# Beta as a row of the matmuls that fill the last stage's accumulators, in place of thirteen additions among the experts

## The chip, the cores and the metric

The kernel runs on one core of a Trainium2 chip. The metric is the device time of one execution in microseconds. It was timed in three runs before the change.

Five engines work beside each other, each through its own queue of instructions in order: TensorE (PE, matrix products into the accumulators of PSUM), VectorE (DVE), ScalarE (ACT), GpSimd (POOL) and SyncE (SP), which in this kernel issues most of the transfers. GpSimd issues the indirect ones (gathers and scattered writes).

## The reference

One layer of a graph network with a mixture of experts, a batch norm, a residual and a layer norm. There are 6250 nodes with 256 features, 200,000 edges and 64 experts.

```
h    = x * rsqrt(deg_out);  m = segment_sum(h[src], dst) * rsqrt(deg_in)
x1   = m @ W_gc + b_gc + (x @ W_res + b_res)
core = top-2 mixture of 64 experts of x1 (gelu between two layers, gates by softmax)
y    = x1 + core
mean, var = of y over the nodes
bn   = (y - mean) * rsqrt(var + 1e-5) * gamma + beta
out  = layernorm(x + bn)          # over the 256 features
```

`beta` has 256 values, one for each feature, and is added to every node's row.

## The kernel before, in words

The nodes stand in NT = 50 tiles of TP = 125 rows. Three parts follow one another: the sum over the edges (about 0 to 930 us of the profiled execution), the experts (about 990 to 1441 us, with the gating ahead of them), and the final stage (to 1544 us).

**The experts' stage.** `slotted()` has one loop over the 64 experts, e = -1 to 63. Iteration e does the first layer of expert e+1, the transposes for e+2 and the second layer of e:

- TensorE makes `ph` from `xgT` and `w1s` (L1647), and ScalarE takes it through gelu into `hT` (L1649).
- Rows of nodes are gathered four experts ahead, into `xg` (GpSimd, L1605). TensorE transposes them into `pte` (L1627), VectorE copies this into `xgT` (L1630), and picks the gates with small instructions `two` (L1636).
- VectorE subtracts `c` from one tile of x1 (`room`, L1758; both inputs lie in SBUF) and adds the tile to `x_sum` (L1759).
- The second layer gives `py` (L1663); VectorE adds the bias (`yb`, L1673). Some experts go by columns: `ph` (L1685), `yT` on VectorE (L1686), `py` (L1692).
- ScalarE scales by the gate (`ys`, L1701, six buffers), VectorE adds to `y_sum` (L1702), and GpSimd writes the rows to `y_dram` at scattered places. The page gives all indirect transfers of this stage one line, L1605; they are told apart by their tiles.
- `ahead(e)` lets SP issue the loads: the next experts' weights (`w1s` L1242, `w2s` L1252, `b2s`; VectorE copies the biases, `bc`, L1244), tiles of x1, and, at e % 4 == 2, four tiles of the kernel's input into `fb` (`node_in`, L212). `fb` holds the residual x for the final stage: 128 partitions by 50 tiles by 256.

At e == 3 SP also brings `beta`, repeated on 125 partitions, into the tile `bet`. From e = 5 on, at e % 4 == 1, GpSimd adds `bet` to the four tiles of `fb` that a load has brought before (L1774), 13 times in all.

The order on TensorE, ScalarE, VectorE and SP is the order in which this stage's code is written. GpSimd's is not: the scheduler puts its instructions in a row, except that all gathers, and each expert's first write, keep the program's order among themselves.

**The final stage.** After the experts, `y_dram` comes back in `yr`, is added to x1 (VectorE), and the sums over nodes give `mean`, `scale` and `less` = mean * scale. `shifted(t, whole)` (L1987) then brings tiles of `fb` into accumulators `pf` by a matmul with the stationary matrix `unit`: the identity in its first 125 rows, and -1 in the rows from 125 on. For the tiles from 12 on, a DMA has put `less`, repeated, into partition 125 of `fb` (L2041), and the matmul reads 126 rows: so pf = fb + beta - less, beta being in `fb` already. For the first 12 tiles the matmul runs ahead of `less`, with 125 rows, and `less` is subtracted by a second one. VectorE adds `pf` to the scaled tiles, and the layer norm follows.

`unit` is made by GpSimd ahead of the experts (L1480 and L1481).

Of the kernel before, what the change touches and what calls it, by code (L numbers as in the profile page):

```python
# [9 lines left out]
F32 = mybir.dt.float32  # L10
# [6 lines left out]
ALU = mybir.AluOpType  # L17
# [9 lines left out]
TP = 125  # L27
NT = N // TP
# [3 lines left out]
D = 256  # L32
# [140 lines left out]
def gnn_moe_kernel(ctx, tc, x_in, x_cols, src, dst, bases, nexts, firsts, parts, lasts, W_gc, b_gc, W_res, b_res, Wg, bg, w1, b1, w2, b2,  # L173
                   gamma, beta, out):
    nc = tc.nc
    V, S, G, T = nc.vector, nc.scalar, nc.gpsimd, nc.tensor
# [6 lines left out]
    def node_rows(ap, t0, n):  # L183
        return ap[t0 * TP:(t0 + n) * TP, :].rearrange("(t p) d -> p t d", p=TP)
# [13 lines left out]
    def node_dma(eng, to_sbuf, tile_ap, rows):  # L198

        for a, b in ((0, 112), (112, TP)):  # L200
            if to_sbuf:
                loads.append(eng.dma_start(out=tile_ap[a:b], in_=rows[a:b]))
            else:
                eng.dma_start(out=rows[a:b], in_=tile_ap[a:b])

    def node_in(tile_ap, ap, t0, n, end=NT):

        if t0 + n in (end, NT):
            node_dma(nc.sync, True, tile_ap[:TP, n - 1:n], node_rows(ap, t0 + n - 1, 1))
            n -= 1  # L210
        if n:
            loads.append(nc.sync.dma_start(out=tile_ap[:, :n], in_=bass.AP(  # L212
                tensor=ap.tensor, offset=ap.offset + t0 * TP * ap.ap[0][0],
                ap=[[ap.ap[0][0], 128], [TP * ap.ap[0][0], n], [1, ap.shape[1]]])))

    def bcast_rows(ap, n):
        return ap.rearrange("(o d) -> o d", o=1).to_broadcast([n, ap.shape[0]])
# [21 lines left out]
    ident = const.tile([128, 128], F32, name="ident")  # L239
# [8 lines left out]
    pidx = const.tile([128, 1], F32, name="pidx")  # L248
# [100 lines left out]
    with tc.tile_pool(name="edges", bufs=1) as ep, ExitStack() as later:  # L349
        iota_h = ep.tile([128, NS * WMAX, 2], FP16, name="iota_h")  # L350
        for a in range(0, NS * WMAX, 128):
            b = min(a + 128, NS * WMAX)
            V.tensor_scalar(iota_h[:, a:b, :], iota_f[:, :b - a, None].to_broadcast([128, b - a, 2]), float(a), None,
                            op0=ALU.add)
# [64 lines left out]
        with tc.tile_pool(name="late", bufs=1) as lp, tc.tile_pool(name="both", bufs=2) as bp, \  # L419
# [33 lines left out]
            for k, w in enumerate((W_gc, W_res)):  # L453
                nc.sync.dma_start(out=wcat[:, :, k * D:(k + 1) * D],
                                  in_=w.rearrange("(k p) d -> p k d", p=128))
# [200 lines left out]
            for i in range(NGR // CG):  # L656
# [55 lines left out]
                if i % 6 == 0 and 6 <= i <= 42:  # L712
                    r = i // 6 * 7
                    nc.sync.dma_start(out=z_dram[0:6272, :].rearrange("(p r) d -> p r d", p=128)[:, r - 7:r, :],
                                        in_=zeros[:, None, :].to_broadcast([128, 7, D + 2]))
# [30 lines left out]
        with tc.tile_pool(name="xs", bufs=1) as xs, tc.tile_pool(name="hotg", bufs=2) as hg, \  # L746
# [417 lines left out]
            now, n = 0.0, 0  # L1164
# [47 lines left out]
    unit = rpool.tile([128, TP], F32, name="unit")  # L1212
    below = rpool.tile([128, 1], F32, name="below")
# [67 lines left out]
    with tc.tile_pool(name="ps_r", bufs=1, space=PSUM) as ps_r, tc.manual_schedule():  # L1281
# [7 lines left out]
        for t0 in range(ta, tb, 4):  # L1289
            n = min(4, tb - t0)  # L1290
# [5 lines left out]
        for t0 in range(0, NL, 4):  # L1296
            n = min(4, NL - t0)
# [135 lines left out]
        for t0 in range(tb, NT, 10):  # L1433
            n = min(10, NT - t0)
# [23 lines left out]
        for k, h in enumerate(HAVE):  # L1458
# [6 lines left out]
                               op1=ALU.mult, accum_out=slots_of)  # L1465
# [11 lines left out]
        G.tensor_copy(dump8, dump[:, :FULL])  # L1477
        G.memset(y_sum, 0.0)
        G.memset(x_sum, 0.0)
        G.tensor_scalar(below, pidx, float(TP), -1.0, op0=ALU.is_ge, op1=ALU.mult)  # L1480
        G.tensor_scalar(unit, ident[:, :TP], below, None, op0=ALU.add)  # L1481
        G.memset(minus, -1.0)

        by_place(1, 0, E)
# [92 lines left out]
    fpool = ctx.enter_context(tc.tile_pool(name="fpool", bufs=1))  # L1577
    fb = fpool.tile([128, NT, D], F32, name="fb")
    gam = fpool.tile([TP, D], F32, name="gam")
    bet = fpool.tile([TP, D], F32, name="bet")  # L1580
    with tc.tile_pool(name="ex", bufs=2) as xp, \
            tc.tile_pool(name="ps_t", bufs=1, space=PSUM) as ps_t, \
            tc.tile_pool(name="ps_h", bufs=4, space=PSUM) as ps_h, \
# [4 lines left out]
        def settled():  # L1588
            while late:
                late.pop(0)()  # L1590
# [19 lines left out]
        def rows_in(idc, m, static=True):  # L1610

            xgs = []
            for k, at in enumerate(idc):
                n = min(128, m - k * 128)
                xg = gx.tile([128, D + 2], F32, name="xg")
                kept(static)(out=xg[:n], out_offset=None, in_=x_dram[:, :],
                             in_offset=bass.IndirectOffsetOnAxis(ap=at[:n], axis=0))
                xgs.append(xg)
            return xgs
# [100 lines left out]
        def columns(tab, e):  # L1720
            c, n, m = _place(turns[e])
            return [tab[:, c + k:c + k + 1] for k in range(n)]

        def turned(e, xgs):
            c, n, m = _place(turns[e])
            return turned_in(xgs, slots_of_turn[e], [mine_of[:, c + k, :] for k in range(n)], columns(gate_of, e),
                             () if e else owners)
# [3 lines left out]
        def slotted():  # L1731

            rows = [rows_in(columns(ids, e), slots_of_turn[e]) for e in range(EARLY)]
            xgTs = [turned(0, rows[0])]
            hTs = []
            for e in range(-1, E):
                if e >= 0:
                    ahead(e)
                if 0 <= e < E - EARLY:
                    rows.append(rows_in(columns(ids, e + EARLY), slots_of_turn[e + EARLY]))  # L1740
                first, second, sides = [], [], []
                if e + 1 < E:
                    hT, first = first_layer(*firsts_of[e + 1], xgTs[e + 1], slots_of_turn[e + 1])
                    hTs.append(hT)
                if e >= 0 and turns[e] in by_columns:
                    sides, second = second_layer_columns(seconds_of[e][0], firsts_of[e][1], hTs[e], columns(dest, e),
                                                         columns(gate_of, e), slots_of_turn[e])
                elif e >= 0:
                    second = second_layer(*seconds_of[e], hTs[e], columns(dest, e), columns(gate_of, e), slots_of_turn[e],
                                          True, e == E - 1)  # L1750
                for run in first[:2]:
                    run()
                    settled()
                if e + 2 < E:
                    xgTs.append(turned(e + 2, rows[e + 2]))
                if 0 <= e < NT:
                    xe = x(tb + e if e < NT - tb else ta + e - NT + tb if e < NT - ta else e - NT + ta)
                    V.tensor_tensor(xe, xe, c0, ALU.subtract)  # L1758
                    V.tensor_tensor(x_sum, x_sum, xe, ALU.add)  # L1759
                if sides:  # L1760
                    n = 1 if len(second) > 2 else 2
                    for run in sides + first[2:2 + n] + second[:2] + first[2 + n:] + second[2:]:
                        run()
                    first, second = [], []
                for k in range(4):
                    for run in second[k:k + 1]:
                        run()
                    for run in first[2 + k:3 + k]:
                        run()
                        settled()  # L1770
                if e % 4 == 1 and e > 4 and e // 4 * 4 - 4 < NT:
                    t0 = e // 4 * 4 - 4
                    n = min(4, NT - t0)
                    G.tensor_tensor(fb[:TP, t0:t0 + n, :], fb[:TP, t0:t0 + n, :],  # L1774
                                    bet[:, None, :].to_broadcast([TP, n, D]), ALU.add)

        def ahead(e):
            if e % 3 == 1 and e // 3 * 3 < ta:
                t0 = e // 3 * 3
                n = min(3, ta - t0)  # L1780
                node_in(x_all(t0, n), x_rows, t0, n, ta)
            if e == 3:
                nc.sync.dma_start(out=bet, in_=bcast_rows(beta, TP))
                nc.sync.dma_start(out=gam, in_=bcast_rows(gamma, TP))
            if e % 4 == 2:
                t0 = e // 4 * 4
                n = min(4, NT - t0)
                if n > 0:
                    node_in(fb[:, t0:t0 + n, :], x_in, t0, n)
            if 2 < e + 2 < E:  # L1790
                r = turns[e + 2]
                seconds_of.append(second_weights(order[0:1, r:r + 1], r not in by_columns))
            if e + 3 < E:
                firsts_of.append(first_weights(order[0:1, turns[e + 3]:turns[e + 3] + 1]))
# [9 lines left out]
    with tc.For_i(0, n_again, 1), tc.tile_pool(name="all", bufs=1) as ap, \  # L1804
# [7 lines left out]
        whole = 2 * N // 128  # L1812
        for r in range(0, whole, 8):
            n = min(8, whole - r)
            nc.sync.dma_start(out=y_dram[0:128 * whole, :].rearrange("(p r) d -> p r d", p=128)[:, r:r + n, :],
                              in_=zeros[:, None, :].to_broadcast([128, n, D]))
# [3 lines left out]
        with tc.For_i(0, n_groups, 1) as gi:  # L1820
# [6 lines left out]
                            op1=ALU.mult)  # L1827
# [3 lines left out]
                                   op0=ALU.mult, op1=ALU.add)  # L1831
# [22 lines left out]
            with tc.For_i(0, n_win, 1):  # L1854
# [17 lines left out]
                                     in_=res, in_offset=None, compute_op=ALU.add)  # L1872
# [100 lines left out]
    with tc.tile_pool(name="fin", bufs=1) as fp, tc.tile_pool(name="gat", bufs=4) as gp, \  # L1973
# [9 lines left out]
        def shifted(t, whole):  # L1983

            pf[t] = ps_f.tile([TP, 2, D], F32, name="pf")
            n = TP + 1 if whole else TP
            T.matmul(pf[t], unit[:n, :], fb[:n, t:t + 2, :], start=True, stop=whole)  # L1987

        pm = ps_m.tile([TP, D], F32, name="pm")
# [3 lines left out]
        for t in range(0, 6, 2):  # L1993
            shifted(t, False)
# [25 lines left out]
        t0 = 0  # L2020
# [16 lines left out]
        less = fp.tile([TP, D], F32, name="less")  # L2037
        V.tensor_mul(less, mean, scale)


        nc.sync.dma_start(out=fb[TP:TP + 1, 12:, :], in_=less[0:1, None, :].to_broadcast([1, NT - 12, D]))  # L2041
        for t in range(0, 12, 2):
            T.matmul(pf[t], minus, less[0:1, None, :].to_broadcast([1, 2, D]), start=False, stop=True)  # L2043

# [1 line left out]
        groups, t0 = [], 0  # L2046
# [113 lines left out]
```

## Time and profile before

| | |
|---|---|
| median of 3 runs | 1558.65 us (1556.74 to 1560.66) |
| profiled execution | 1545.78 us |
| its span | 1544.1 us |
| mean granted clock of TensorE | 0.957 |
| TensorE, VectorE, ScalarE, GpSimd busy | 1374.5, 1094.7, 802.1, 790.0 us |
| TensorE's idle time, 990 to 1441 us | 31.6 us (the sum over its lines) |
| additions of `bet` to `fb` (L1774) | 13, 29.5 us of GpSimd, from 1009.8 to 1357.9 us |

The durations in the text come from the profiled execution; the result will stand against the median of the runs, 12.9 us (0.8%) above it. Rows of the timeline give start and duration, then the engine, line, operation and tiles; the bracket at their end is the engine's idle time before the row and what ended it. Rows of the groups give total, mean duration and the idle time before. Rows of the waits give total, count and longest.

### The profile page before, as it was taken

The page shows a single profiled execution, that of the slowest core. Times are in us where ns is not written, and L with a number is a line of the kernel's source. Part 1 is how long each engine was busy: PE and PEld are TensorE (multiplying, and loading weights), DVE is VectorE, ACT ScalarE, POOL GpSimd, SP SyncE. Part 2 cuts the span into 40 slices and gives each one's busy share as a digit, 9 for nine tenths or more (in the row PEclk, how much of TensorE's full clock was granted, in tenths as well). Part 3 has the DMA queues.
Part 4 walks back from the last instruction along what each step waited for, and adds up shares of the span by engine and source line. Part 5 has one row for each costly group of instructions (what it writes and reads, how often), then busy time and mean ns, then how long its engine had stood idle before and what let it go on. Part 6 is the DMA issues. An engine that isn't in the chain of part 4 may idle for free. (4 is left out here: it accounts for less than half of the span.)

```text
span 1544.1 us, 32496 instructions
## 1 busy us (share of the span) xinstructions
PE 1374.5 (89%) x9814; PEld 1143.0 (74%) x9814; DVE 1094.7 (71%) x3328; ACT 802.1 (52%) x2127; POOL 790.0 (51%) x900
## 2 busy tenths in 40 slices
PE   8998577899999999999999987799999988998783
PEld 4555466777888989899999985688778877787541
DVE  9999976888888877777767579455544455433587
ACT  7887634567766666565555534333333333333258
POOL 4000256776676667666676632366556666554100
PEclk9999688999999999999999999999999999999897
DMA  6765856666677777777777747688797866576645
GB/s 199 210 210 158 315 167 187 195 193 194 182 205 217 197 218 204 202 216 212 224 201 200 199 133 197 157 252 264 231 279 236 252 212 212 187 222 209 220 161 156
DMA packets 197857, 319.84 MB, mean 207 GB/s; under 512 B 27245, under 2 KB 129442, under 8 KB 197673
## 3 DMA queue, kind: packets, MB, share of 16 engines
q1 hardware_dynamic: 143308, 170.57, 35.2%
q0 software_dynamic: 47888, 146.88, 33.2%
q10 hardware_dynamic: 6477, 0.24, 0.6%
q8 instruction: 79, 1.29, 0.3%
q14 instruction: 105, 0.86, 0.2%
HBM read 250.79 MB, written 60.35 MB: 202 GB/s over the span
## 5 line engine op out<-in xcount | busy, mean ns | idle before, releaser
L766 POOL DMA_INDIRECT r<-h_dram,srcg x445 | 481.2, 1081 | 259.6 <-PE pc L857 90.2
L912 PE MATMUL sm<-hrow,room 128*128 128x258 f32 x1470 | 492.3, 349 | 8.9 <-DVE room L900 7.3
L877 ACT CAST room<-pc 128x196 f32 (+7 forms) x879 | 356.6, 406 | 221.1 <-PE pc L857 117.6
L913 PE MATMUL sm<-hrow,room 128*128 128x256 f32 x1470 | 397.1, 283 | 0.0
L857 PE MATMUL pc<-hotk,lo 128*128 128x245 bf16 (+7 forms) x1118 | 308.3, 308 | 42.3 <-issue 16.4
L835 DVE TENSOR_TENSOR hotk<-key,iota_h 128x784 bf16<-128x784 f16 (+4 forms) x488 | 248.0, 508 | 136.0 <-PE pc L857 90.0
L912 PEld LDWEIGHTS sm<-hrow,room 128*128 128x128 f32 x1470 | 289.5, 197 | 27.4 <-issue 18.7
L913 PEld LDWEIGHTS sm<-hrow,room 128*128 128x128 f32 x1470 | 282.2, 192 | 1.3
L1649 ACT ACTIVATE hT<-ph,bc 128x112 f32<-128x112 f32 (+16 forms) x256 | 106.0, 425 | 286.6 <-PE ph L1647 143.2
L1647 PE MATMUL ph<-xgT,w1s 128*128 128x112 f32 (+17 forms) x1024 | 208.0, 348 | 9.6 <-ACT hT L1649 4.7
L900 DVE TENSOR_TENSOR room<-pc,room 128x49 f32 x908 | 197.0, 239 | 18.5 <-issue 6.2
L1647 PEld LDWEIGHTS ph<-xgT,w1s 128*128 128x128 f32 x1024 | 171.2, 198 | 31.8 <-issue 10.0
L1605 POOL DMA_INDIRECT y_dram<-ys,dest x124 | 120.0, 968 | 145.5 <-ACT ys L1701 101.5
L1605 POOL DMA_INDIRECT xg<-x_dram,ids x124 | 118.5, 956 | 83.6 <-issue 66.8
L771 PE MATMUL pg<-r,hot 128*128 128x258 f32 x445 | 146.9, 330 | 11.5 <-ACT resg L1154 5.0
L857 PEld LDWEIGHTS <-lo 128*128 128x128 bf16 x1118 | 100.7, 102 | 72.2 <-issue 16.5
L1630 DVE TENSOR_SCALAR xgT<-pte,bsum 128x112 f32<-128x112 f32 (+14 forms) x128 | 48.7, 421 | 111.7 <-PE pte L1627 40.1
L772 PE MATMUL pg<-r,hot 128*128 128x256 f32 x445 | 126.6, 285 | 0.0
L1663 PE MATMUL py<-w2s,hT 128*128 128x256 f32 (+3 forms) x424 | 107.0, 396 | 7.0 <-DVE y_sum L1702 4.1
L771 PEld LDWEIGHTS pg<-r,hot 128*128 128x128 f32 x445 | 86.9, 195 | 23.4 <-issue 11.4
L1685 PE MATMUL ph<-hT,w2s 128*128 128x208 f32 (+9 forms) x480 | 98.9, 358 | 2.2 <-issue 1.7
L384 DVE TENSOR_TENSOR lo<-lo_b,iota 128x1024 bf16<-128x1024 bf16 x140 | 96.0, 686 | 5.1 <-PE pc L857 4.4
(373 smaller groups left out, 2006.2 us busy)
## 6 DMA issues: line engine op xcount, KB each, us to landing
w1s<-in_L_gnn_w_dram SPq DMA_DIRECT2D x64, 512.0 KB
w2s<-in_L_gnn_w_dram SPq DMA_DIRECT2D x64, 512.0 KB
yr<-y_dram SPq DMA_DIRECT2D x10, 1024.0 KB
h_dram<-hrow SPq DMA_DIRECT2D x5, 1536.0 KB
r<-h_dram,srcg POOLq DMA_INDIRECT x445
f<-in_x_cols_dram SPq DMA_DIRECT2D x25, 256.0 KB
z_dram<-zeros SPq DMA_DIRECT2D x7, 903.0 KB
r_dram<-hx SPq DMA_DIRECT2D x24, 256.0 KB
```

The source lines that it names most:

```text
L766: G.indirect_dma_start(out=f32(r[:, :2 * D]), out_offset=None, in_=h_dram[:, :], in_offset=bass.IndirectOffsetOnAxis(ap=idx, axis=0))
L771: T.matmul(pg, hot, r[:, D:], start=first, stop=False)
L772: T.matmul(pg[:, :D], hot, r[:, :D], start=False, stop=last)
L835: V.tensor_tensor(hot, pairs(key, e, n, m), iota_h[:, None, :m, :].to_broadcast([128, n // 2, m, 2]), ALU.is_equal)
L857: T.matmul(pc, los[g // PAIRS][:, r // 2, :, r % 2], hots.pop(g), start=(i == 0), stop=(i == k - 1))
L877: put = S.copy(counts[c % 2][:, :, 1:][:, :, ds(at, w - 1)], pc[:, :, 1:])
L900: add = V.tensor_tensor(to, more, f32(had), ALU.add).ins
L912: T.matmul(sm, by, hrow[:, t, D:], start=(t == 0), stop=False)
L913: T.matmul(sm[:, :D], by, hrow[:, t, :D], start=False, stop=(t == NS - 1))
L1605: w = G.indirect_dma_start(**kw)
L1647: T.matmul(ph[:, :m], w1s[:, kk, c * 128:(c + 1) * 128], xgT[:, kk, :m], start=(kk == 0), stop=(kk == 1))
L1663: T.matmul(py[:n], hT[:, c, k * 128:k * 128 + n], w2s[:, c, :], start=(c == 0), stop=(c == 3))
```

## The change

`beta` becomes a row of `fb`, beside the shift's row. `unit` gets a row of +1 at 125 and -1 from 126 on, beside the identity; since `ident` has no entry in its 125 columns there, it is now made of a comparison and an addition. At e == 53, after the last load of `fb`, SP copies `beta` fifty times into partition 125. The shift's row `less` goes to partition 126. The matmuls read 126 rows for the first 12 tiles and 127 for the others. The tile `bet`, its load and the 13 additions go.

```diff
-        G.tensor_scalar(below, pidx, float(TP), -1.0, op0=ALU.is_ge, op1=ALU.mult)
-        G.tensor_scalar(unit, ident[:, :TP], below, None, op0=ALU.add)
+        G.tensor_scalar(below, pidx, float(TP + 1), -2.0, op0=ALU.is_ge, op1=ALU.mult)
+        G.tensor_scalar(unit, pidx.to_broadcast([128, TP]), float(TP), below, op0=ALU.is_ge, op1=ALU.add)
+        G.tensor_tensor(unit, unit, ident[:, :TP], ALU.add)
...
-    bet = fpool.tile([TP, D], F32, name="bet")
...
-                if e % 4 == 1 and e > 4 and e // 4 * 4 - 4 < NT:
-                    t0 = e // 4 * 4 - 4
-                    n = min(4, NT - t0)
-                    G.tensor_tensor(fb[:TP, t0:t0 + n, :], fb[:TP, t0:t0 + n, :],
-                                    bet[:, None, :].to_broadcast([TP, n, D]), ALU.add)
...
             if e == 3:
-                nc.sync.dma_start(out=bet, in_=bcast_rows(beta, TP))
                 nc.sync.dma_start(out=gam, in_=bcast_rows(gamma, TP))
...
+            if e == NT + 3:
+                nc.sync.dma_start(out=fb[TP:TP + 1], in_=beta[None, None, :].to_broadcast([1, NT, D]))
...
-            n = TP + 1 if whole else TP
+            n = TP + 2 if whole else TP + 1
...
-        nc.sync.dma_start(out=fb[TP:TP + 1, 12:, :], in_=less[0:1, None, :].to_broadcast([1, NT - 12, D]))
+        nc.sync.dma_start(out=fb[TP + 1:TP + 2, 12:, :], in_=less[0:1, None, :].to_broadcast([1, NT - 12, D]))
```

The order of the instructions on TensorE, VectorE and ScalarE stays as it was. GpSimd's changes in the experts' stage. Before, around the second addition:

```order
L1605 DMA xg<-x_dram,ids 128x258 x2
L1605 DMA xg<-x_dram,ids 96x258
L1605 DMA xg<-x_dram,ids 128x258
L1605 DMA xg<-x_dram,ids 112x258
L1605 DMA y_dram<-ys,dest 28372x256
L1774 TENSOR_TENSOR fb<-fb,bet 125x1024
L1605 DMA y_dram<-ys,dest 28372x256 x2
```

Now, at the same place (`xg` rows are gathers, `y_dram` rows the experts' scattered writes):

```order
L1605 DMA xg<-x_dram,ids 128x258 x2
L1605 DMA xg<-x_dram,ids 96x258
L1605 DMA y_dram<-ys,dest 28372x256
L1605 DMA xg<-x_dram,ids 128x258
L1605 DMA xg<-x_dram,ids 112x258
L1605 DMA y_dram<-ys,dest 28372x256 x2
```

The addition is gone, and one write that stood behind two gathers now stands ahead of them. Over the stage 12 gathers have one or two more writes ahead of them than before, and some 55 have fewer. A later place on the same engine, as a difference:

```order
 L1605 DMA xg<-x_dram,ids 112x258
+L1605 DMA y_dram<-ys,dest 28372x256 x2
 L1605 DMA xg<-x_dram,ids 128x258
 L1605 DMA xg<-x_dram,ids 48x258
-L1774 TENSOR_TENSOR fb<-fb,bet 125x1024
-L1605 DMA y_dram<-ys,dest 28372x256 x6
+L1605 DMA y_dram<-ys,dest 28372x256 x4
```

Two of six writes that came in a row behind the addition have moved ahead of two gathers.

SP's queue has one entry less at e == 3 and one more at e == 53, `fb<-beta`, between two weight loads:

```order
L1242 DMA w1s<-in_L_gnn_w_dram 128x2x512
L1785 DMA fb<-in_L_gnn_beta_dram 1x50x256
L1249 TENSOR_LOAD order
L1252 ISA
L1252 DMA w2s<-in_L_gnn_w_dram 128x4x256
```

The copy stands directly ahead of the next expert's load of `w2s`.

## The prediction

> **What bounds the kernel now.** I read the page's head first, then the stretches of the program, then the groups of the lines that the change touches, and last the rows around each addition.
>
> ```profile
> span 1544.1 us, 32496 instructions
> PE 1374.5 (89%) x9814; PEld 1143.0 (74%) x9814; DVE 1094.7 (71%) x3328; ACT 802.1 (52%) x2127; POOL 790.0 (51%) x900
> core 0: us, PE busy (x) PEld busy (x) DVE busy (x) ACT busy (x) POOL busy (x), PEclk, DMA share, GB/s
> 1050.00:1110.00 60.00, 59.84 (x289) 47.35 (x288) 30.87 (x99) 21.37 (x49) 36.23 (x35) 1.00 0.76 242
> 1290.00:1350.00 60.00, 52.99 (x290) 42.95 (x289) 30.01 (x101) 19.31 (x48) 32.83 (x33) 0.97 0.60 191
> ```
>
> TensorE is busy in 89% of the span. The two lower rows (windows of the span; after the length, busy time by engine) lie in the experts' stage, where all the additions are: in the first stretch TensorE hardly pauses, in the second it loses 7 of 60 us, VectorE and GpSimd work about half the time, and the transfers take 60 to 76%. So an instruction taken off GpSimd helps only if TensorE waited for it, directly or through another engine.
>
> ```profile
> L1774 POOL TENSOR_TENSOR fb<-fb,bet 125x1024 f32<-125x1024 f32 (+1 forms) x13 | 29.5, 2271 | 9.1 <-DMA fb<-in_x_dram 7.7 <-issue 1.2
> POOL y_dram L1605 <- ACT ys L1701: 101.5, 40, 7.0
> 1440.62 3.08 DMA y_dram<-ys,dest
> ```
>
> The 13 additions hold GpSimd for 29.5 us. But in the same stage GpSimd waits 101.5 us, in 40 places, for ScalarE's `ys`: its queue is in step with the results, not behind. The chain that ended last runs, from the experts on, through the last write of `y_dram`, which GpSimd can't issue before the last expert's `ys` exists. Taken by themselves the additions are hidden by these 101.5 us.
>
> **What the additions do to VectorE.** The stretch behind the second addition:
>
> ```profile
> 1034.15 0.15 DVE L1636 SCALAR_TENSOR_TENSOR two<-xg,mine_of 128x2 f32<-128x2 f32 x1
> 1034.22 3.31 DVE L1758 TENSOR_TENSOR room<-room,c 125x256 f32<-125x256 f32 x1
> 1034.87 2.37 POOL L1774 TENSOR_TENSOR fb<-fb,bet 125x1024 f32<-125x1024 f32 x1
> 1037.91 0.42 DVE L1673 TENSOR_TENSOR yb<-py,b2s 128x256 f32<-128x256 f32 x1
> 1038.38 1.63 PE L1663 MATMUL py<-w2s,hT 128*128 128x256 f32 x3 [1.11 <-DVE yb L1673]
> ```
>
> The subtraction of `c`, whose two inputs both lie in SBUF, takes 3.31 us and ends 0.3 us after the addition; undisturbed it takes 0.42 (1265.91 below). VectorE stood still for 2.9 us, `yb` came late, and TensorE waited 1.11 us for it. The tenth addition:
>
> ```profile
> 1263.60 2.36 POOL L1774 TENSOR_TENSOR fb<-fb,bet 125x1024 f32<-125x1024 f32 x1
> 1264.19 1.79 DVE L1636 SCALAR_TENSOR_TENSOR two<-xg,mine_of 112x2 f32<-112x2 f32 x1
> 1265.91 0.42 DVE L1758 TENSOR_TENSOR room<-room,c 125x256 f32<-125x256 f32 x1
> 1266.71 0.73 DVE L1686 TENSOR_SCALAR yT<-ph,bc 128x192 f32<-128x192 f32 x2
> 1267.17 1.23 PE L1692 MATMUL py<-ident,yT 128*128 128x128 f32 x4 [3.48 <-DVE yT L1686]
> ```
>
> Here a `two` takes 1.79 us instead of 0.15, so 1.64 of TensorE's wait of 3.48 is the standstill's; the other 1.84 has another cause. Other standstills reach nobody:
>
> ```profile
> 1009.70 2.52 DVE L1636 SCALAR_TENSOR_TENSOR two<-xg,mine_of 128x2 f32<-128x2 f32 x1
> 1010.77 1.03 PE L1647 MATMUL ph<-xgT,w1s 128*128 128x256 f32 x4
> 1289.89 2.77 DVE L1244 COPY bc<-bT 128x6 f32 x1
> 1292.97 0.47 DVE L1702 SCALAR_TENSOR_TENSOR y_sum<-py,gate_of,y_sum 32x256 f32<-32x256 f32 x1 [0.32 <-ACT ys L1701]
> ```
>
> During the first, TensorE runs on without a wait (no bracket at 1010.77); after the second, VectorE itself waits for ScalarE soon, so it had caught up.
>
> **What else stands beside the additions.** Not every gap there is theirs:
>
> ```profile
> 1116.37 0.46 SPq L212 DMA_DIRECT2D fb<-in_x_dram  x1
> 1121.04 0.45 ACT L1649 ACTIVATE hT<-ph,bc 128x224 f32<-128x224 f32 x1 [1.53 <-PE pte L1627]
> 1125.14 2.35 POOL L1774 TENSOR_TENSOR fb<-fb,bet 125x1024 f32<-125x1024 f32 x1
> 1127.31 2.95 PE L1647 MATMUL ph<-xgT,w1s 128*128 128x224 f32 x7 [2.37 <-ACT hT L1649]
> 1208.58 2.00 PE L1663 MATMUL py<-w2s,hT 128*112 128x256 f32 x5 [2.02 <-DVE y_sum L1702]
> ...
> 1100.00:1110.00 10.00, 10.00 (x57) 8.91 (x56) 5.40 (x16) 3.99 (x10) 6.11 (x7) 1.00 0.48 166
> 1117.00:1127.00 10.00, 7.95 (x49) 7.02 (x47) 1.86 (x6) 2.03 (x6) 8.15 (x8) 1.00 0.98 318
> ```
>
> Each addition works on four tiles of `fb` that one load has brought shortly before; here SP issued it 8.8 us ahead of the addition. After the load the DMA engines are full (0.98 against 0.48), VectorE and ScalarE fall to 2 us of work in ten, and `hT` is already late at 1121.04, four microseconds before the addition. That load stays, so I count the 2.37 at 1127.31 and, by the same picture, the 2.02 at 1208.58 to the transfers. The clock is the last piece (columns: the window, its length, PE busy, granted clock, share of the DMA engines, GB/s):
>
> ```profile
> 1038.40:1041.80 3.40, 3.40 (x8) 0.51 0.81 259
> 1127.20:1130.60 3.40, 3.29 (x10) 0.50 1.03 333
> 1209.10:1212.50 3.40, 3.40 (x10) 0.50 0.53 195
> 1267.10:1270.50 3.40, 3.33 (x17) 0.50 0.83 305
> 1304.70:1308.10 3.40, 3.36 (x14) 0.50 0.74 235
> 1359.30:1366.10 6.80, 6.28 (x23) 0.50 0.53 185
> ```
>
> These six windows at half the granted clock each follow a wait of TensorE; 1304.7 has no addition near it. TensorE is busy all through them, so a window of 3.40 us costs 1.7.
>
> **The change, part by part.**
> - The additions go: 29.5 us of GpSimd, nothing on the path but the standstills. Term: −1.1 (1034) and −1.64 (1263), together −2.7. The rest I take at nothing, for the two reasons shown (TensorE has queued work, or VectorE has slack).
> - The half-clock windows: behind the gap of 1.11 at 1038.38, which goes whole, the window should go: −1.7. At 1267.17 a wait of 1.84 remains, longer than the 1.11 that sufficed at 1038, so I leave that window in place. Bounds 0 and −3.4. The Trainium skill ("TensorE: Matmul & The Clock Gate", "HAM oscillation — how this bites in real kernels") asks only that TensorE have no idle gap above some 3.4 us; by that a gap of 1.11 couldn't halve the clock, and this term would be nothing, with a sum of about −2.7. The trace differs: the half clock begins at 1038.40, right behind the 1.11, and I follow the trace.
> - The load of `bet` (125 rows of 1 KB) goes; the row of `beta` (50 pieces of 1 KB) comes in at iteration 53. Both lie among transfers that leave the DMA engines room (0.60 to 0.76 above), and the row is needed only a stage later, where its semaphore has long been counted up. Taken as nothing. For the bounds I let the load's issue (0.39, below) and the shift's (0.73, the nearest row to a copy into one partition) stand on SP's path: −0.4 to +0.7.
> - `unit` takes one GpSimd instruction more, at most as long as the one before (0.64, below), in the preparation ahead of the experts. GpSimd's next task there is descriptors for the first gathers; cover is TensorE's remaining work of that stage. Nothing; upper bound +0.6.
> - The matmuls read one more row each:
>
> ```profile
> L1987 PE MATMUL pf<-fb,unit x50: 592/592/1217, 1447.6 to 1525.0; 126*125 126x512 f32 x38, 125*125 125x512 f32 x12
> L1783 SPq DMA_DIRECT2D bet<-in_L_gnn_beta_dram x1: 393/393/393, 999.7 to 999.7; - x1
> L2041 SPq DMA_DIRECT2D fb<-less x1: 727/727/727, 1492.3 to 1492.3; - x1
> L1481 POOL TENSOR_SCALAR unit<-ident,below x1: 636/636/636, 934.5 to 934.5; 128x125 f32<-128x125 f32 x1
> ```
>
>   125 and 126 rows together have a lowest and a middle duration of 592 ns, so the row is free: 0. The shift's row moves from partition 125 to 126 with the same 38 pieces: 0.
> - GpSimd's queue is put in another order: without the additions its writes of `y_dram` and gathers of `xg` stand differently to each other. Twelve gathers have one or two more writes ahead of them, some fifty fewer. Behind such a write, which waits for ScalarE, the gather waits too, and behind the gather TensorE's transposes (`pte`). Taken as nothing on this row:
>
> ```profile
> PE pte L1627 <- DMA xg<-x_dram,ids: 0.2, 1, 0.2
> ```
>
>   TensorE waited for a gather once, 0.2 us, in the whole stage; they are issued four experts ahead. The other end is the rival below.
>
> Sum: −2.7 − 1.7 = −4.4. The profiled execution took 1545.78 us with the 1.7 around its span, and would come to 1541.4. It lies 12.9 us under the median of the runs, 1558.65, which is what the result will be held against; the stage's gain is the same there, so 1558.65 − 4.4 = 1554.3.
>
> **The rivals.**
> - *More than the two standstills* (larger gain). All the gaps at the additions are theirs, since VectorE's backlog lasts longer than the trace tells: 1.11 + 3.48 + 2.37 + 2.02 = 9.0 from the rows above, and five of the windows (all but 1304.7), 4 × 1.7 + 3.4 = 10.2: up to −19, about 1539.5; with half of it −9.6, 1549. For it: five windows lie right behind additions. Against: `hT` was late before the addition came, and at 1127 no VectorE instruction ran beyond its length.
> - *Nothing.* The stage is paced by the transfers, and what TensorE no longer waits for VectorE, it waits for weights or `hT` some matmuls later: 1558.65, within 2. For it: the 1.84 left at 1267, and the DMA share of 0.98 behind the load at 1116. Against: in the stretch 1050 to 1110 the transfers leave a quarter free and TensorE doesn't wait.
> - *Slower, through GpSimd's new order.* A write that stands ahead of a gather waits 101.5/40 = 2.5 us in the mean, 7.0 at most. If the twelve gathers were late by it and a third came through to `pte`, that is 4 × 2.5 = 10 us, less the −4.4 of the standstills: +5.6, 1564; with none of the gain, +10, 1568.7. It decides from the point where a gather lands after its transposes could start, of which the 0.2 us is so far the only sign.
>
> **How the numbers follow.** Chances: the forecast (−1 to −7: from the 1.1 alone to 2.7 + 3.4 + 0.4) 0.50, more 0.20, nothing 0.15, slower 0.12, something not thought of 0.03. The likeliest case's own range is 1551.7 to 1557.7. For 8 in 10 I leave out the far half of the larger gain (below 1542) and most of the slower case (above 1563): 1542 to 1563. What a measurement can tell from no change is 0.3%, 4.7 us. The forecast's centre lies just inside; some 0.4 of its chance is beyond it: 0.20 for faster, with 0.20 from the larger gain: 0.40. Within: 0.30 + 0.15 + 0.02 = 0.47. Slower: 0.12 and 0.01.
>
> **What would show it.** Right: no `room`, `two` or `bc` on VectorE above 1 us in the stage; no wait for `yb` near 1038, no half clock there; the waits behind the loads of `fb` (near 1127, 1208) still there; PE's wait for `xg` still under 1 us. Wrong: these waits gone too (then they were the additions'), waits of `pte` for `xg` of several microseconds (GpSimd's order), or a new gap elsewhere that takes back the 4.4.

## The result, and the profile after

The changed kernel took 1551.61 us in the median of 12 runs (1541.18 to 1557.15), the kernel before 1558.39 in 12 runs on the same chip. The ratio is 0.9941, with a 95% interval of 0.9924 to 0.9958: 9.2 us faster, between 6.5 and 11.8 (the two medians alone differ by 6.8 us, inside this interval). The forecast was 4.4 us.

The profiled execution of the changed kernel doesn't show this gain. Here are its head and its experts' stage (first matmul of the first layer to the last of the second; columns as in the prediction's windows), and below them, for comparison, that stage before:

```profile
span 1552.2 us, 32482 instructions
PE 1375.7 (89%) x9814; PEld 1142.5 (74%) x9814; DVE 1081.4 (70%) x3328; ACT 800.9 (52%) x2127; POOL 758.5 (49%) x888
987.00:1449.00 462.00, 426.04 (x2316) 361.62 (x2316) 211.98 (x780) 152.54 (x380) 234.79 (x244) 0.97 0.73 227
```

```profile
980.00:1440.00 460.00, 426.95 (x2316) 363.22 (x2316) 226.20 (x780) 152.62 (x380) 263.54 (x257) 0.97 0.72 228
```

GpSimd has lost 28.8 us of work in the stage and VectorE 14.2, yet the stage lasts 2 us longer. Single executions scatter by more than the effect (1541 to 1557 after, 1553 to 1564 before), and this pair lies the wrong way round: the profiled execution of before took 12.6 us less than its median, and less than any of its 12 runs; that of after took 2.2 us more than its own. So the pair shows what became of each instruction, and only the runs give the sum.

What became of the instructions is as forecast. The three groups of VectorE, with mean durations in the second column of the right half:

```profile
L1758 DVE TENSOR_TENSOR room<-room,c 125x256 f32<-125x256 f32 x50 | 20.8, 416 | 0.0
L1636 DVE SCALAR_TENSOR_TENSOR two<-xg,mine_of 128x2 f32<-128x2 f32 (+7 forms) x124 | 14.3, 151 | 0.0
L1244 DVE COPY bc<-bT 128x6 f32 x61 | 11.2, 184 | 2.4 <-issue 1.0
```

```profile
L1758 DVE TENSOR_TENSOR room<-room,c 125x256 f32<-125x256 f32 x50 | 23.7, 473 | 0.0
L1636 DVE SCALAR_TENSOR_TENSOR two<-xg,mine_of 128x2 f32<-128x2 f32 (+7 forms) x124 | 23.1, 222 | 0.0
L1244 DVE COPY bc<-bT 128x6 f32 x61 | 14.8, 243 | 2.3 <-ACT hT L1649 0.5 <-issue 0.4
```

After stands above, before below: 15.3 us of standstill (2.9 + 8.8 + 3.6) are gone. No `room`, `two` or `bc` of the stage takes more than 0.44 us now, and TensorE waits for no gather (`xg`) there. The small parts of the change, and TensorE's waits after:

```profile
L1983 PE MATMUL pf<-fb,unit x50: 590/592/1217, 1456.7 to 1532.9; 127*125 127x512 f32 x38, 126*125 126x512 f32 x12
L1785 SPq DMA_DIRECT2D fb<-in_L_gnn_beta_dram x1: 882/882/882, 1376.9 to 1376.9; - x1
L1481 POOL TENSOR_SCALAR unit<-pidx,below x1: 752/752/752, 937.4 to 937.4; 128x125 f32<-128x125 f32 x1
L1482 POOL TENSOR_TENSOR unit<-unit,ident x1: 447/447/447, 938.2 to 938.2; 128x125 f32<-128x125 f32 x1
PE py L1692 <- DVE yT L1686: 13.1, 10, 3.3
PE ph L1647 <- ACT hT L1649: 8.1, 6, 3.5
```

The longer matmuls take 592 ns as before. The copy of `beta` is issued in 0.88 us, and no row shows a wait for it. TensorE's waits for `yT` and `hT` are no smaller than before (10.9 and 4.7 there).

### The profile page after: what moved, and what is told of

Read it like the earlier page. It is cut to its first block, busy times and chain, and to the rows that moved or that the text cites. A ratio compares the mean times of both kernels' runs of the same rounds, so it can differ in the third digit from the quotient of the medians.

```text
span 1552.2 us, 32482 instructions
## 1 busy us (share of the span) xinstructions
PE 1375.7 (89%) x9814; PEld 1142.5 (74%) x9814; DVE 1081.4 (70%) x3328; ACT 800.9 (52%) x2127; POOL 758.5 (49%) x888
## 5 line engine op out<-in xcount | busy, mean ns | idle before, releaser
L766 POOL DMA_INDIRECT r<-h_dram,srcg x445 | 475.3, 1068 | 269.6 <-PE pc L857 91.8
L857 PE MATMUL pc<-hotk,lo 128*128 128x245 bf16 (+7 forms) x1118 | 307.9, 307 | 45.1 <-issue 15.3
L771 PE MATMUL pg<-r,hot 128*128 128x258 f32 x445 | 147.2, 331 | 12.5 <-issue 5.8
L609 PE MATMUL pr<-room,f 128*128 128x512 f32 x196 | 99.3, 631 | 0.0
```

The costliest lines, as they stand in the source:

```text
L766: G.indirect_dma_start(out=f32(r[:, :2 * D]), out_offset=None, in_=h_dram[:, :], in_offset=bass.IndirectOffsetOnAxis(ap=idx, axis=0))
L771: T.matmul(pg, hot, r[:, D:], start=first, stop=False)
L857: T.matmul(pc, los[g // PAIRS][:, r // 2, :, r % 2], hots.pop(g), start=(i == 0), stop=(i == k - 1))
```

## The experiments

The kernels went to the chips in three groups, each group with the kernel before beside it on the same chip. The kernel before took 1541.8 us in the first group, 1451.0 in the second and 1450.4 in the third. Each group ran on another chip, and ratios hold within a group.

### First group (kernel before: 1541.8 us)

**Without the additions.**

```diff
-                    G.tensor_tensor(fb[:TP, t0:t0 + n, :], fb[:TP, t0:t0 + n, :],
-                                    bet[:, None, :].to_broadcast([TP, n, D]), ALU.add)
```

> The kernel before without its 13 additions on GpSimd; bet is still loaded, beta is not added at all (that part of the computation is left out), and the final matmuls stay as they were. GpSimd's order among the experts is that of the changed kernel. Theory S (VectorE's standstills beside the additions are the cost): as much faster as the change itself, ratio to before 0.990 to 0.997, VectorE's busy time in 990 to 1441 us lower by about 15 us. Theory O (the new order and the free time of GpSimd are the gain): the same ratio, since order and free time are the same. Theory R (the gain is from the rest: bet's load, the tile's place, the longer matmuls): ratio 1.000 within 0.002.

Measured: 0.9948 (0.9928 to 0.9968), 8.0 us faster. The missing additions give the change's whole gain within the intervals, though the change itself was timed on another chip; theory R (the rest of the change) falls.

**Memsets in their place.**

```diff
-                    G.tensor_tensor(fb[:TP, t0:t0 + n, :], fb[:TP, t0:t0 + n, :],
-                                    bet[:, None, :].to_broadcast([TP, n, D]), ALU.add)
+                    for _ in range(2):
+                        G.memset(fb[:TP, t0:t0 + n, :], 0.0)
```

> The kernel before with each addition replaced by two GpSimd memsets of the same four tiles of fb to zero: GpSimd is still held at the same places behind the same loads, but reads nothing in SBUF (the residual is left out of the output). Its order stays nearly that of before. Theory S: no room, two or bc on VectorE above 1 us, and faster as the change is, ratio 0.990 to 0.997. Theory O: as slow as before, 0.998 to 1.002, since GpSimd's order and work are those of before. If memsets too stop VectorE, its busy time tells: about 15 us more than in the run without additions.

Measured: 0.9971 (0.9953 to 0.9988), 4.5 us faster. Its window and its groups:

```profile
978.00:1435.00 457.00, 425.69 (x2316) 362.60 (x2316) 212.81 (x779) 152.27 (x380) 259.29 (x270) 0.97 0.73 229
L1758 DVE TENSOR_TENSOR room<-room,c 125x256 f32<-125x256 f32 x50 | 20.8, 416 | 0.0
L1636 DVE SCALAR_TENSOR_TENSOR two<-xg,mine_of 128x2 f32<-128x2 f32 (+7 forms) x124 | 14.4, 152 | 0.0
```

GpSimd works nearly as long as before (259.3 against 263.5 us), with the same order of gathers and writes, and VectorE hardly stands still any more (212.8 against 226.2). The kernel is faster all the same, so theory O alone (order and free time) falls; the ratio lies at the upper edge of what theory S expected (0.997). The Trainium skill ("SBUF — State Buffer", "Who interferes with whom") states that a VectorE instruction with two inputs in SBUF contends with a GpSimd instruction that reads SBUF, not with one that only writes it. The traces agree for `room` and `two`, which have two inputs: in the mean they take 416 and 152 ns beside the memsets, 473 and 222 beside the additions. One `bc`, a copy with a single input, still took 1.38 us beside the memsets, against 2.77 at most before and 0.42 without additions. Whether the 3.5 us between this run and the one before it are the order, GpSimd's time or nothing, the two intervals don't tell.

**The additions twice.**

```diff
+                    for _ in range(2):
                     G.tensor_tensor(fb[:TP, t0:t0 + n, :], fb[:TP, t0:t0 + n, :],
                                     bet[:, None, :].to_broadcast([TP, n, D]), ALU.add)
```

> The kernel before with each addition done twice (beta enters doubled). Theory S with the change's gain of 0.6%: the same price again, ratio 1.003 to 1.009, VectorE's busy time in the stage higher by 10 to 20 us, and TensorE waits for yb or yT right behind. By the sum of the prediction (4.4 us): 1.001 to 1.004. Theory O or R: 1.000 within 0.002, as GpSimd waits over 70 us for ScalarE in any case.

Measured: 1.013 (1.0103 to 1.0157), 20.0 us slower, more than any theory had it.

```profile
977.00:1455.00 478.00, 429.83 (x2318) 363.37 (x2316) 241.46 (x780) 152.70 (x380) 295.92 (x271) 0.97 0.70 219
PE py L1692 <- DVE yT L1686: 16.6, 10, 3.8
PE py L1663 <- DVE y_sum L1702: 4.9, 3, 2.4
PE py L1663 <- DVE yb L1673: 3.3, 3, 1.5
```

VectorE's work in the stage is 211.6 us without additions, 226.2 with one set (the profile of before, from another chip), 241.5 with two. The first 14.6 us of it cost 8.0 us of time, the next 15.3 cost 20.0 (15.9 to 24.2). So the price isn't a fixed part of the standstill. It isn't GpSimd's longer queue either: the waits for `yT` and `yb`, both from VectorE, are longer (10.9 and 1.7 us before), while TensorE waits for a gather once in the stage, for 0.3 us. Part of the price in these profiles is clock: the same matmuls keep TensorE busy 6.3 us longer than in the kernel without additions (429.8 against 423.5, its window below), with eight spells of 3.4 us at half clock instead of five. That the price grows because the slack is used up fits this, but one profile of each kernel doesn't prove it.

**Loads of `fb` one tile at a time** (in the changed kernel).

```diff
-            if e % 4 == 2:
-                t0 = e // 4 * 4
-                n = min(4, NT - t0)
-                if n > 0:
-                    node_in(fb[:, t0:t0 + n, :], x_in, t0, n)
+            if 0 <= e < NT:
+                node_in(fb[:, e:e + 1, :], x_in, e, 1)
```

> The changed kernel with the loads of fb one tile in each of 50 iterations instead of four in every fourth. Theory T (TensorE's waits near 1127, 1183, 1209 and 1359 belong to the 512 KB loads): they shrink, faster than the changed kernel by 4 to 10 us, ratio to before 0.985 to 0.992, and TensorE's idle time between 990 and 1441 us falls from 34 to under 27 us. If these waits were not the loads': ratio as the changed kernel's, 0.992 to 0.996, and the idle time stays above 30 us.

Measured: 0.9975 (0.9957 to 0.9993). It isn't faster than the change (0.9941, on another chip) or than the kernel without additions on the same chip (0.9948); its middle lies above both expected ranges. Its stage:

```profile
975.00:1427.00 452.00, 421.11 (x2316) 358.31 (x2316) 211.62 (x780) 151.89 (x380) 236.53 (x244) 0.98 0.74 231
```

TensorE still idles for 30.9 us of it, as in the kernel without additions (30.5, below). Theory T, by which the waits near 1127 and 1209 belong to the large loads of `fb`, falls: loads of a quarter of the size leave the idle time as it was. The bytes stayed the same, so this speaks of the loads' size alone. A stretch of the kernel without additions shows such a wait with neither an addition nor a load of `fb` near (the last one was issued at 1268.99, the next at 1299.39):

```profile
973.00:1427.00 454.00, 423.50 (x2316) 360.19 (x2316) 211.56 (x779) 151.76 (x380) 235.85 (x244) 0.98 0.73 231
...
1290.00:1292.00 2.00, 2.00 (x17) 1.93 (x17) 1.11 (x3) 0.83 (x2) 1.39 (x3) 1.00 1.08 404
1292.00:1294.00 2.00, 2.00 (x12) 1.69 (x11) 0.03 (x1) 0.41 (x1) 1.55 (x2) 1.00 0.53 170
1294.00:1296.00 2.00, 1.43 (x10) 1.13 (x8) 0.00 (x0) 0.41 (x1) 1.54 (x2) 1.00 0.27 91
1296.00:1298.00 2.00, 0.00 (x0) 0.00 (x0) 0.07 (x1) 0.00 (x0) 0.34 (x1) 1.00 0.26 66
```

The DMA engines were full from 1290 to 1292 (1.08). From 1296 to 1298 nearly everything stands still, with the DMA engines at 0.26.

### Second group (kernel before: 1451.0 us)

**The changed kernel again.**

> The changed kernel once more, for a second profile and a ratio beside the other kernels of this group. Ratio 0.992 to 0.997. If its experts' stage was 461 us in the first profile by that execution's disturbance alone, it takes 450 to 457 us here.

Measured: 1.0007 (0.9991 to 1.0022), outside what was expected. On this chip the change does nothing, and the stage takes 414 us instead of the 450 to 457 expected. The profile suggests why:

```profile
span 1443.6 us, 32482 instructions
927.00:1341.00 414.00, 409.20 (x2316) 354.65 (x2316) 214.08 (x780) 152.88 (x380) 236.84 (x244) 0.99 0.81 253
```

TensorE idles for 4.8 us of the stage instead of 36, and behind the stage's first 5 us no half clock is left. There is next to no wait in the stage that a shorter VectorE could end.

**The changed kernel with the order of before** on GpSimd.

```diff
+                if e % 4 == 1 and e > 4 and e // 4 * 4 - 4 < NT:
+                    t0 = e // 4 * 4 - 4
+                    n = min(4, NT - t0)
+                    G.tensor_scalar(fb[:TP, t0:t0 + n, 0:1], fb[:TP, t0:t0 + n, 0:1], 0.0, None, op0=ALU.add)
```

> The changed kernel with a GpSimd instruction on 4 columns (adding 0.0 to one feature of four tiles) at the places where the additions stood; it keeps the order of gathers and writes of the kernel before. It separates GpSimd's order from the rest. Theory S (the standstills alone): the changed kernel's time within 0.2%. Theory L (the new order, in which 29 of 125 gathers stand behind one to three more writes than before, costs something that the standstills' end pays for): faster than the changed kernel by 0.2 to 0.5%. Theory O (the new order is a gain): slower than the changed kernel by 0.2 to 0.5%.

Measured: 1.0000 (0.9987 to 1.0012). Here the order is worth nothing either way; with TensorE nearly without waits this says little about the slower chips.

**Small memsets in place of the additions.**

```diff
-                    G.tensor_tensor(fb[:TP, t0:t0 + n, :], fb[:TP, t0:t0 + n, :],
-                                    bet[:, None, :].to_broadcast([TP, n, D]), ALU.add)
+                    G.memset(fb[:TP, t0:t0 + n, 0:1], 0.0)
```

> The kernel before with each addition replaced by a memset of 4 columns on GpSimd at the same place behind the same load (output without beta, one feature's residual zeroed). Order and waits of GpSimd as before, its 29.5 us and the standstills gone. Theory S: ratio as that of the kernel without additions, 0.992 to 0.997. Theory O: 0.998 to 1.002.

Measured: 0.9994 (0.9984 to 1.0005): no change. Neither expected case can be told apart on a chip where the additions cost nothing.

**Additions of one tile.**

```diff
-                    G.tensor_tensor(fb[:TP, t0:t0 + n, :], fb[:TP, t0:t0 + n, :],
-                                    bet[:, None, :].to_broadcast([TP, n, D]), ALU.add)
+                    for t in range(t0, t0 + n):
+                        G.tensor_tensor(fb[:TP, t, :], fb[:TP, t, :], bet, ALU.add)
```

> The kernel before with each addition of four tiles split into four of one tile each: the same work, order of gathers and writes as before. If VectorE stands still for the whole of the instruction that it meets, its longest two, room or bc falls from 2.5 to 3.3 us to under 1.1, while the sum of the overruns may stay at 10 to 18 us; where the price is in the length of one standstill (slack is used up), ratio 0.994 to 0.998; where it is in the sum, 0.998 to 1.003.

Measured: 0.9993 (0.9983 to 1.0004). The standstills are there, though shorter for `two` (0.75 us at most) and `room` (1.01), as expected; not for `bc`:

```profile
934.00:1348.00 414.00, 409.75 (x2316) 354.82 (x2316) 226.62 (x779) 153.15 (x380) 272.64 (x294) 0.99 0.81 253
1219.77 2.77 POOL L1775 TENSOR_TENSOR fb<-fb,bet 125x256 f32<-125x256 f32 x4
1219.37 3.21 DVE L1244 COPY bc<-bT 128x6 f32 x1
1222.49 0.47 DVE L1702 SCALAR_TENSOR_TENSOR y_sum<-py,gate_of,y_sum 32x256 f32<-32x256 f32 x1
```

VectorE works 226.6 us, 12.5 more than in the changed kernel beside it, and once stands still for 3 us, and the stage lasts the same 414 us. So VectorE's overruns are there on this chip too; what is absent is anyone who waits for them.

### Third group (kernel before: 1450.4 us)

This chip turned out as that of the second group, so the runs answer only that half of what was expected.

> The changed kernel a third time. Theory C (the additions' price hangs on the chip: where TensorE runs the experts' stage without waits, in about 413 us, VectorE's standstills are hidden; where the stage takes 450 to 460 us with some 30 us of waits, they show): ratio 0.999 to 1.002 if the stage takes under 420 us, 0.992 to 0.997 if it takes over 445. Theory K (the gain of 0.6% in the first comparison was chance between runs): 0.998 to 1.002 in both cases.

Measured: 1.0004 (0.9987 to 1.0022), with a stage of 413 us; as theory C has it, and here theory K has the same.

> The additions done twice, again. Theory C: where the stage takes under 420 us, much less than the 1.3% of the first time, ratio 1.000 to 1.006, as the double standstill of 4.7 us is longer than what TensorE has queued only here and there; where it takes over 445, again 1.010 to 1.016. Theory K: 1.010 to 1.016 in both cases.

Measured: 1.0056 (1.0037 to 1.0076), 8.1 us slower, against 20.0 in the first group. The ratio is the one that theory C expected, and K falls: the two intervals lie apart.

```profile
930.00:1351.00 421.00, 410.73 (x2316) 353.97 (x2316) 246.26 (x780) 153.11 (x380) 297.65 (x271) 1.00 0.79 249
L1759 DVE TENSOR_TENSOR x_sum<-x_sum,room x50: 424/426/2851, 937.3 to 1273.5; 125x256 f32<-125x256 f32 x50
PE py L1663 <- DVE yb L1673: 1.4, 1, 1.4
```

VectorE works 246.3 us, 32 more than in the changed kernel of the group before, and single instructions run to 3.1 us. The stage lasts 7 us longer (421 against 414).

> The kernel before with 4-column memsets in place of the additions: GpSimd's order and waits as before, no standstills (output without beta, one feature's residual zeroed). Where the stage takes over 445 us: theory S (the standstills are the price there) 0.992 to 0.997, as the changed kernel; theory O (the new order of GpSimd is the gain there) 0.998 to 1.002. Where it takes under 420 us: 0.999 to 1.001 by both.

Measured: 0.9996 (0.9979 to 1.0012): no change, as in the second group.

> Four additions of one tile in place of each of four tiles, same work. Where the stage takes over 445 us: if the length of one standstill is the price, 0.994 to 0.998; if the sum of the standstills (14 us, measured) is, 0.998 to 1.003. Where it takes under 420 us: 0.999 to 1.001.

Measured: 1.0013 (0.9998 to 1.0029): just outside what was expected at its middle, inside with its interval. With the 0.9993 of the second group it can't be told from no change.

No version gained more on the kernel before than the change itself.

## Why the prediction was right, and where not

- *The standstills of VectorE are the mechanism.* Right: they go with the additions (15.3 us), they nearly go with memsets that hold GpSimd almost as long, they double in sum with doubled additions, and the time follows on the chips of the first result and the first group. That the number came inside the range is partly luck with the chip: on the chips of the other two groups the change is worth nothing. The prediction had that as a rival, but for another reason, and without a word of the chip.
- *Their price, −2.7, is the mis-sized term.* The whole gain was 9.2 us (6.5 to 11.8) on the chip of the first result, above the forecast's −1 to −7; the additions alone measured 8.0 (4.9 to 11.1) on that of the first group. I had counted the two waits with a frozen instruction in front of them and set all others at nothing, because TensorE had queued work or VectorE slack. The two counted waits fell by 3.3 us (the 1.11 is gone, and the 3.48 became the 1.32 below), so what is missing lies in the ones set at nothing. On a chip where some 30 us of other waits may use that slack, this cover is thin; the second set of additions (20 us for 15.3) points the same way. Which of the further waits the standstills lengthen, the single profiles don't show.
- *The clock, −1.7.* Open. In the changed kernel the stretch where 1038 was has no half clock and no wait, and a half clock still follows the wait for `yT` that stands where 1267 was, both as forecast:

```profile
1038.00:1050.00 12.00, 12.00 (x69) 1.00 1.07 361
1185.60:1189.00 3.40, 3.40 (x14) 0.51 0.96 349
1274.20:1277.60 3.40, 3.40 (x18) 0.53 0.90 321
...
1273.41 0.76 PE L1692 MATMUL py<-ident,yT 128*128 128x128 f32 x3 [1.32 <-DVE yT L1686]
```

  But others have come at other places (1185.6). Behind the stage's first microseconds there are seven spells of 3.4 us before (the double one at 1359 counts as two) and six after. One fewer is what the term says, but only two of the six stand where one stood before, so one pair of executions can't credit it to the change. The half clock at 1274 again begins right behind a wait of 1.32 us. A short wait alone doesn't bring it, though: with the additions done twice in the third group, TensorE waited 1.43 us (until 964.1) and 1.97 us (until 1226.8), and ran on at a granted clock of 1.00.
- *The waits belong to the loads of `fb`.* Wrong as far as their size goes, by the kernel with single-tile loads, and wrong for the wait at 1296. By the prediction's own sign, too, the waits near 1127 and 1208 should have stayed. At the same places of the changed kernel the first is smaller (1.15 instead of 2.37) and the second gone (no bracket):

```profile
1135.94 1.75 PE L1647 MATMUL ph<-xgT,w1s 128*128 128x224 f32 x8 [1.15 <-ACT hT L1649]
1216.00 1.98 PE L1663 MATMUL py<-w2s,hT 128*112 128x256 f32 x8
```

  That could speak for the additions, but waits of the same size have come at other places (at 1356.12, 2.17 us for `yT`), so one pair of executions doesn't tell. What makes these waits on some chips is not settled. It isn't a property of the program alone: the same program runs without them on others.
- *The rest at nothing.* Right: no row waits for the copy of `beta` or for `unit`, the longer matmuls cost 0, and the kernel without additions but otherwise as before has the change's gain, on another chip and within the intervals. The copy's issue took 0.88 us, above the 0.73 that I took as its nearest row.
- *GpSimd's new order.* The described order was miscounted ahead of the prediction. Counted along the whole queue, 29 of some 125 gathers stand behind one to three more writes than before (12 behind one, 16 behind two, one behind three), and none behind fewer. The rival built on it, a slower kernel, fell: the changed kernel is 9.2 us faster, and TensorE waits for no gather. On the chips without waits the order is worth nothing (order of before in the changed kernel: 1.0000). On the others it wasn't tried apart: the 3.5 us between the memsets and no additions could hold a small gain or nothing.
- *The rivals "more" and "nothing".* In time, each fits some chips. The measured 9.2 is the half price of the first (−9.6); whether by its mechanism, a backlog of VectorE longer than the trace tells, stays open, as the waits near 1127 and 1208 do. The second holds where TensorE has no waits, and the reason that I gave against it (TensorE doesn't wait in 1050 to 1110) was in truth a reason for it: on the chips where TensorE hardly waits, one set of standstills cost nothing that these runs can measure.

## What to carry to other kernels

An engine that stands still costs only what its slack doesn't cover, and the slack may differ from one chip or occasion to the next: a price measured on one is not the kernel's. When an effect is smaller than the scatter between executions, one profile before and one after tell which instructions changed, and timed runs without the cause tell its price; runs with the cause doubled show whether price and cause are in proportion. And a wait that follows a transfer in time is not shown to be the transfer's until the transfer has been changed.

## What the runs showed of the hardware that I had not expected

- The kernel before took 1558.4 us in the first comparison and 1541.8 in the first group, but 1451.0 and 1450.4 on the chips of the other two, 6 to 7% less. No chip is known to have run twice, so chip and occasion can't be told apart. For the changed kernel the experts' stage takes 462 us in the first comparison and 414 in the second group; the difference is TensorE's idle time (36 against 4.8 us) and busy time (426.0 against 409.2, granted clock 0.97 against 0.99). A small instruction of SyncE tells the two apart as well, by min, median and max in ns between 1000 and 1300 us. The first row is the kernel before, the second the changed kernel of the second group; the changed kernel of the first comparison shows 3 to 725.

```profile
L1252 SPq MOVE w2s<-in_L_gnn_w_dram x42: 3/29/697, 1001.1 to 1296.7; - x42
L1252 SPq MOVE w2s<-in_L_gnn_w_dram x46: 29/29/35, 1004.3 to 1295.1; - x46
```

  The cause of these differences stays open.
- The copy of six columns (`bc`) stood still through all four short additions of one tile, 3.21 us, while the longest `two` fell to 0.75 us: splitting GpSimd's work let some of VectorE's instructions in between, and others not.
